# A small convolution on TensorE: two streams in four slots, or in three with half-height tiles

## The chip, the cores and the metric

The kernel runs on one core of a Trainium2 chip. The metric is the time of one execution on the device in microseconds (us), as the median over runs. TensorE multiplies matrices, VectorE (DVE), ScalarE (ACT) and GpSimd (POOL) do the elementwise work, SyncE (SP) issues most transfers. All data is float32.

## The reference, cut to what matters

`x` is 4 images of 128 channels, 96 x 96. They are group-normalised, and each image is read as four sequences of L = 9216 positions: by columns (V) and by rows (H), each forwards and backwards. Each sequence goes through the same block:

```python
t = grouped1x1(x, in_proj_w, in_proj_b, 4);  u, gate = t[:, :256], t[:, 256:]
u = conv1d(silu(u), dw_w, K=5)                 # depthwise, per channel
s = ssm_in_w @ u                               # 32 rows
a = clip(DMIN + (DMAX - DMIN) * sigmoid(ssm_delta_w @ u + b), ...)
bb, cc = tanh(ssm_b_w @ u + b), tanh(ssm_c_w @ u + b)
h = linear recurrence  h[n] = a[n] * h[n-1] + bb[n] * s[n]
u = u + ssm_out_w @ (cc * h + d * s)
u = grouped1x1(u * sigmoid(gate), mix_w, mix_b, 4)
y = out_proj_w @ u + out_proj_b
```

The four results are put back in image order, fused by a 128 x 512 matrix, and added to `x`.

## The kernel before

**Cut into pieces.** For each image there are two phases, V and then H (8 phases in all), and in each the forward and the backward sequence run together: stream f is s = 0, stream r is s = 1. A phase has NS = 6 steps, and a step four pairs: positions are taken modulo R = 4, and pair p holds the N = 384 positions of a step with remainder p, for both streams. So there are 192 pairs, t = 0 to 191, with p = t % 4. After them six `last_pair` calls empty the pipeline. The order of work on TensorE, VectorE, ScalarE and GpSimd is the order in which the program writes it; each engine takes its own list in that order and waits where its operands are not there.

**One pair, before.** `pair(t)` works on three ages of data at once:

- `rows`, twice: the first product for a unit of the next step (into the banks FRONT) and the gate product for a unit six pairs old (GATE). Tiles of the array are 32x32, sixteen side by side (eight for each purpose). ScalarE then makes the gate's tanh (L354) and the silu (L365).
- `taps`: the 5-tap convolution for the second half of the channels (j = 1). Tap 0 is a scaled copy on ScalarE into PSUM (L424), taps 1 to 4 are on VectorE (L426), both streams in one instruction.
- `conv(i, s)`, once for each stream: the same convolution for the first half of the channels, j = 0. These are laid out with the four remainders across the partitions, 32 channels each, in four groups g. The product with a banded 128x32 matrix for each g does all taps: k = 0 takes the remainders of this block of four positions, k = 1 those of the next. ScalarE copies the result to `u` (L410).
- `recurrence`: in the pairs with p = 0 and 1 half a step's scan on VectorE (L477); in every pair GpSimd makes an older pair's `z = cc * h + d * s` (L483 to L485, a product, a sum, a copy to the other partitions).
- `ssm_out`, `add_u` (L393), `gating` (L398, once for each stream): 32x32 products into the four banks 0 to 3, then VectorE adds `u` and multiplies by the gate.
- `proj(i)`: sixteen 128x32 products for bb, cc, a and s into two banks, then ScalarE: tanh for bb and a (L452), tap 0 of the next pair (L424), tanh for cc (L456), a copy of s (L458), s times d (L459); then GpSimd: two steps for a (L462, L463), bb * s (L464).
- `accumulate`, twice: mixing, output and fusing matrix in one (`w_fin`) on a finished unit, and VectorE adds the result into the image sum `acc` (L504 in V; in H L509 for f, which adds the bias too, and L511 for r). In the usual case the first call of a pair handles f, the second r. At the end of an image the sum is written out (L516) and the next image loaded (L521).

On TensorE a pair's order is: `rows`, `accumulate`, `conv` f, `rows`, `conv` r, `ssm_out`, `proj`, `accumulate`. All products are recorded under one line, L126 of the helper `mm`; they are told apart by their operands. A product in float32 is two instructions (two passes). PSUM has eight banks; which call uses which is fixed by the constants below. `conv` f and the second bank of `proj` share bank 5.

```python
SSM, TAPS, GATE, FRONT = 0, 0, (2, 3), (6, 7)
Y_1, CONV_F, CONV_R, PROJ, Y_2, SMALL = 4, 5, 4, (6, 5), 4, 7
```

At the start GpSimd builds the band matrices (32 products, L281). In the first six pairs no unit is old enough for the gate, `ssm_out` and `accumulate`.

Of the kernel before, what the change touches and what calls it, by code (L numbers as in the profile page):

```python
# [53 lines left out]
def conv_preact_kernel(  # L56
# [100 lines left out]
    NSC = L // SC  # L157
    stats = {}

    def stats_of(b):  # L160
# [4 lines left out]
    def stats_finish(b, newton):  # L165

        mv = sp.tile([P, 2], F32, tag="mv", name=f"mv_{b}")
        nc.vector.bn_aggr(mv, stats[b].rearrange("p c s -> p (c s)"))
        yield
        pm = bank(SMALL)  # L170
# [10 lines left out]
        pv = bank(SMALL)  # L181
# [20 lines left out]
        pb = bank(SMALL)  # L202
# [62 lines left out]

    band = wp.tile([P, R, 2, 4, 32], F32, name="band")
    w_fin = wp.tile([P, 4, 2, P], F32, name="w_fin")
    b_fin = wp.tile([P, 1], F32, name="b_fin")
    with tc.tile_pool(name="prep", bufs=1) as pp:
        w_dw = load(dw_v, [P, 4, 8], "w_dw", pp)  # L270
# [6 lines left out]
        for p in range(R):  # L277
            for k in range(2):
                for g in range(4):
                    m = R * k - p + R - 1  # L280
                    nc.gpsimd.tensor_scalar_mul(  # L281
                        band[:, p, k, g, :], id32, w_dw[:, g, m : m + 1]
                    )

# [40 lines left out]

    def rows(i, bi, banks=(FRONT, GATE)):

# [12 lines left out]
        for c in range(4):  # L340
            for j in range(2):
                if i is not None:
                    r = slice(32 * j, 32 * j + 32)
                    m, q = (c, g) if j else (g, c)
                    mm(bank(banks[0][j]), c, wn[r, 32 * m : 32 * m + 32], x_in[s][r, q, :],
# [17 lines left out]
        if i is not None:  # L363
# [7 lines left out]
            if g == 3:  # L371
                for j in range(2):
                    if un["st"] == 0:
                        r, q = (slice(0, P), slice(0, 2)) if j else (slice(0, 64), slice(0, 4))
                        nc.gpsimd.memset(sil[r, j, q, 0:1], 0.0)
                    if un["st"] == NS - 1:
                        r, q = (slice(0, P), slice(2, 4)) if j else (slice(64, P), slice(0, 4))
                        nc.gpsimd.memset(sil[r, j, q, N : N + 1], 0.0)
# [22 lines left out]

    def conv(i, s):

        un = units[i]
        sil = sils[un["step"]][:, s]
        pc = bank(CONV_R if s else CONV_F)
        for k in range(2):
            for g in range(4):
                mm(pc, g, band[:, un["p"], k, g, :], sil[:, 0, g, k : k + N], k == 0, k == 1)
        nc.scalar.copy(us[i][:, s, 0, :], pc[:, :N])  # L410

# [25 lines left out]

    def proj(i):

# [7 lines left out]
        for j in (1, 0):  # L447
            for bk, cols in zip(PROJ, ((qb, qb, qa, qa), (qc, qc, qs, qs))):
                for c in range(4):
                    mm(bank(bk), c, w_proj[:, j, cols[c]], us[i][:, c % 2, j, :], j == 1, j == 0)  # L450
        pa, pb = (bank(bk)[:, :N] for bk in PROJ)
        nc.scalar.activation(ta[:, p, :], pa, AF.Tanh, bias=b_proj[:, 0:1])  # L452
        if i + 2 < NU:
            new_u(i + 2)
            taps(i + 2, range(1))
        nc.scalar.activation(tb[0:64, p, :], pb[0:64, :], AF.Tanh, bias=b_proj[0:64, 1:2])  # L456
        st = wk.tile([P, N], F32, tag="s", name=f"s_{i}")
        nc.scalar.copy(st[0:64, :], pb[64:P, :])  # L458
        nc.scalar.activation(tb[64:P, p, :], pb[64:P, :], AF.Copy, scale=d_sb[64:P, :])  # L459
        a = ta[64:P, p, :]  # L460
        half = (DMAX - DMIN) / 2
        nc.gpsimd.tensor_scalar(a, a, half, DMIN + half, ALU.mult, ALU.add)  # L462
        nc.gpsimd.tensor_scalar(a, a, 0.9999, 0.0001, ALU.min, ALU.max)  # L463
        nc.gpsimd.tensor_mul(ta[0:64, p, :], st[0:64, :], ta[0:64, p, :])  # L464

    def scan(step, part):
# [4 lines left out]
        if part:  # L471
            init = ta[0:64, R - 1, N // 2 - 1 : N // 2]
        elif units[step * UB]["st"] == 0:
            init = 0.0
        else:
            init = scans[step - 1][0][0:64, R - 1, N - 1 : N]
        nc.vector.tensor_tensor_scan(  # L477
            seq[0:64, r], seq[64:P, r], seq[0:64, r], init, ALU.mult, ALU.add
        )

    def outputs(step, p):
        ta, tb = scans[step]
        nc.gpsimd.tensor_mul(ta[64:P, p, :], tb[0:64, p, :], ta[0:64, p, :])  # L483
        nc.gpsimd.tensor_add(tb[64:P, p, :], ta[64:P, p, :], tb[64:P, p, :])  # L484
        nc.gpsimd.tensor_copy(tb[0:64, p, :], tb[64:P, p, :])  # L485

    reload = []

    def accumulate(bu, bk):
        b, s, p, st = bu["b"], bu["s"], bu["p"], bu["st"]  # L490
        py = bank(bk)
        for j in range(2):
            for c in range(4):
                mm(py, c, w_fin[:, bu["dir"], j, 32 * c : 32 * c + 32], bu["v"][:, j, :],
                   j == 0, j == 1)
        y = py[:, :N]
        if s:
            y, p, st = y[:, ::-1], R - 1 - p, NS - 1 - st
        if bu["order"] == "V":
# [3 lines left out]
            y = y.rearrange("p (c r m) -> p m r c", r=R, m=M)  # L503
            nc.vector.tensor_add(part, y, part)  # L504
            return
        part = acc[:, bass.ts(st, LN), p, :]
        y = y.rearrange("p (h m) -> p h m", m=M)
        if s == 0:
            nc.vector.scalar_tensor_tensor(part, y, b_fin, part, ALU.add, ALU.add)  # L509
        else:  # L510
            nc.vector.tensor_add(part, y, part)  # L511
        if bu["st"] >= NS // 2 and bu["p"] == R - 1:
# [23 lines left out]
    def pair(t):  # L536
        i, k, bi = 2 * t, t % R, 2 * (t - LAG)
        front = i + UB if i + UB < NU else None
        back = bi if bi >= 0 else None
        rows(front, back)  # L540
        taps(i, range(1, 3))

        if waiting and (bi == 2 or (bi - 2) % (NU // B)):
            accumulate(waiting.pop(0), Y_1)
            if len(waiting) > 1 and units[bi]["st"] == 1:
                accumulate(waiting.pop(0), CONV_F)
# [12 lines left out]
        if back is not None:  # L559
            ssm_out(bi)  # L560
            add_u(bi)
            gating(bi, 0)
            if later:
                next(later[0], None)
            gating(bi, 1)
        proj(i)
        if waiting:
            accumulate(waiting.pop(0), Y_2)
        if back is not None:
# [108 lines left out]
```

## Time and profile before

| | |
|---|---|
| median of 3 runs | 2188.05 us (2185.58 to 2188.55) |
| the profiled execution | 2188.14 us, its span 2186.4 us |
| granted TensorE clock | 0.99 |
| instructions | 83167 |
| transfers | 133.84 MB, mean 61 GB/s |

The span runs from the first to the last instruction that the profiler recorded; the execution's own time is a little longer. Where the profile gives rows of the timeline, the first number is the start in us from the span's start, the second the duration in us; then engine, line, operation, what is written <- what is read, the tile's shape on the array (for products), operand shapes, and how many instructions were merged into the row. `[0.96 <-ACT ...]` is idle time of that engine ahead of the row, and what ended it. In rows of groups the figures are count, busy us in total, mean ns of one, and idle time ahead. "us" without a unit in the text below is microseconds.

### The profile page before, as it was taken

What the parts mean: (1) busy time and instruction counts of PE and PEld (TensorE: products, weight loads), DVE (VectorE), ACT (ScalarE), POOL (GpSimd) and SP (SyncE); (2) the same over time, 40 slices, a digit from 0 to 9 for tenths busy, and PEclk for the clock granted to TensorE, in tenths of its full rate; (3) what the DMA queues carried; (4) which work ended last, traced back from release to release, by engine and by line L of the source; (5) the groups of instructions that cost most, each with busy time, mean ns of one, the idle gap of its engine ahead of it and who ended that gap; (6) DMA issues with size and microseconds to landing.
All of it is one profiled execution on the core that took longest, in us unless ns stands there. A gap on an engine that the chain in (4) does not pass through costs nothing.

```text
span 2186.4 us, 83167 instructions
## 1 busy us (share of the span) xinstructions
PE 2136.5 (98%) x37072; PEld 724.7 (33%) x37072; DVE 1871.7 (86%) x1978; ACT 1576.3 (72%) x2899; POOL 1267.8 (58%) x1301
## 2 busy tenths in 40 slices
PE   5899999999999999999999999999999999999998
PEld 3233333333333333333333333333333333333333
DVE  3589998888888988888899899888888888888886
ACT  3677777777777777777777777777777777777762
POOL 2355656566655665666656565656566566655653
PEclk7899999999999999999999999999999999999999
DMA  5122121111441221111333221111134211111111
GB/s 154 39 57 64 49 57 35 42 35 45 141 134 50 56 57 48 36 42 35 100 107 114 57 64 42 41 36 42 35 100 135 55 36 43 35 42 35 35 49 68
DMA packets 83398, 133.84 MB, mean 61 GB/s; under 512 B 11616, under 2 KB 70624, under 8 KB 83040
## 3 DMA queue, kind: packets, MB, share of 16 engines
q1 hardware_dynamic: 81024, 127.64, 21.6%
q8 instruction: 291, 4.77, 0.9%
q10 hardware_dynamic: 2016, 0.88, 0.2%
q14 instruction: 67, 0.55, 0.1%
HBM read 109.60 MB, written 18.87 MB: 59 GB/s over the span
## 4 chain that ended last, share of the span: by engine, by line
PE 95%; DVE 2%; ACT 1%; DMA 1%; issue 1%; POOL 0%; ACTq 0%; SPq 0%; DVEq 0%
PE psum L126 95%; DVE psum L393 0%; DMA acc<-in_xr 0%; DVE gv L398 0%; DMA b_mix<-in_mix_b 0%; ACT psum L424 0%; ACT t L459 0%; DVE t L477 0%; ACT sil L365 0%; ACT gv L354 0%; DMA w_in<-in_in_wT 0%; DVE acc L511 0%; ACT t L452 0%; DVE psum L426 0%; ACT s L458 0%
## 5 line engine op out<-in xcount | busy, mean ns | idle before, releaser
L426 DVE SCALAR_TENSOR_TENSOR psum<-sil,w_tap,psum 128x768 f32<-128x768 f32 x576 | 585.7, 1017 | 49.6 <-ACT psum L424 42.2
L126 PE MATMUL psum<-sil,band 128*32 128x384 f32 x6144 | 576.7, 492 | 12.7 <-ACT t L459 10.4
L126 PE MATMUL psum<-gv,w_fin 128*32 128x384 f32 x6144 | 569.8, 490 | 0.5 <-DVE gv L398 0.5
L126 PE MATMUL psum<-u,w_proj 128*32 128x384 f32 x6144 | 536.0, 489 | 0.0
L462 POOL TENSOR_SCALAR t<-t 64x384 f32<-64x384 f32 x192 | 190.5, 992 | 568.7 <-ACT t L452 564.8
L354 ACT ACTIVATE gv<-psum,bnorm 128x384 f32<-128x384 f32 x768 | 403.1, 577 | 134.6 <-PE psum L126 129.9
L393 DVE TENSOR_TENSOR psum<-psum,u 128x1536 f32<-128x1536 f32 x192 | 339.2, 1767 | 170.4 <-PE psum L126 122.1
L452 ACT ACTIVATE t<-psum,b_proj 128x384 f32<-128x384 f32 x192 | 194.4, 1013 | 373.2 <-PE psum L126 373.2
L365 ACT ACTIVATE sil<-psum,bnorm 128x385 f32<-128x385 f32 x768 | 404.7, 586 | 18.0 <-PE psum L126 17.8
L126 PE MATMUL psum<-x_in,wn 32*32 32x384 f32 (+1 forms) x12288 | 405.8, 499 | 8.5 <-ACT t L452 3.0
L483 POOL TENSOR_TENSOR t<-t,t 64x384 f32<-64x384 f32 x192 | 235.6, 1227 | 220.0 <-DVE t L477 205.8
L398 DVE SCALAR_TENSOR_TENSOR gv<-gv,psum 128x768 f32<-128x768 f32 x384 | 350.8, 950 | 6.3
L126 PEld LDWEIGHTS psum<-sil,band 128*32 128x32 f32 x6144 | 181.0, 109 | 361.0 <-issue 218.8
L126 PEld LDWEIGHTS psum<-gv,w_fin 128*32 128x32 f32 x6144 | 181.7, 110 | 342.1 <-issue 222.7
L126 PEld LDWEIGHTS psum<-u,w_proj 128*32 128x32 f32 x6144 | 181.8, 110 | 335.1 <-issue 225.9
L464 POOL TENSOR_TENSOR t<-s,t 64x384 f32<-64x384 f32 x192 | 238.2, 1240 | 15.0 <-ACT s L458 0.7
L484 POOL TENSOR_TENSOR t<-t,t 64x384 f32<-64x384 f32 x192 | 235.3, 1226 | 15.1
L410 ACT COPY u<-psum 128x384 f32<-128x384 f32 x384 | 186.8, 487 | 44.9 <-PE psum L126 28.2
L126 PEld LDWEIGHTS psum<-x_in,wn 32*32 32x32 f32 x12288 | 115.5, 103 | 271.0 <-ACT sil L365 118.1
L426 DVE SCALAR_TENSOR_TENSOR u<-sil,w_tap,psum 128x768 f32<-128x768 f32 x192 | 194.9, 1015 | 6.8
L463 POOL TENSOR_SCALAR t<-t 64x384 f32<-64x384 f32 x192 | 191.4, 997 | 15.9
L126 PE MATMUL psum<-t,w_so 32*32 32x384 f32 x6144 | 188.9, 494 | 0.0
(70 smaller groups left out, 1204.5 us busy)
## 6 DMA issues: line engine op xcount, KB each, us to landing
x_in<-in_xs SPq DMA_DIRECT2D x96, 385.0 KB, 4.4
x_in<-in_xs SPq DMA_DIRECT2D x384, 96.2 KB, 2.4
acc<-in_xr SPq DMA_DIRECT2D x48, 384.0 KB, 4.3
out<-acc SPq DMA_DIRECT2D x48, 384.0 KB, 2.9
xs<-in_xr SPq DMA_DIRECT2D x72, 192.0 KB, 2.7
w_fuse<-in_fuse_wT ACTq DMA_DIRECT2D x1, 256.0 KB, 6.8
w_proj<-in_proj_wT ACTq DMA_DIRECT2D x1, 128.0 KB, 4.9
w_so<-in_ssm_out_wT ACTq DMA_DIRECT2D x1, 128.0 KB, 2.6
```

Source lines behind the costliest of these rows:

```text
L126: nc.tensor.matmul(o[r, : rhs.shape[-1]], lhsT, rhs, start=start, stop=stop, skip_group_check=True)
L354: nc.scalar.activation(gv[:, j, :], bank(banks[1][j])[:, :N], AF.Tanh, bias=gbn[:, 2 + j : 3 + j], scale=0.5,)
L365: nc.scalar.activation(sil[:, j, g, :], bank(banks[0][j])[:, : N + 1], AF.Silu, bias=bn[:, 1:2] if j else bn[:, 4 + g : 5 + g],)
L393: nc.vector.tensor_add(pz, pz, us[bi].rearrange("p s j n -> p (s j) n"))
L398: nc.vector.scalar_tensor_tensor(v, v, 1.0, pz, ALU.add, ALU.mult)
L426: nc.vector.scalar_tensor_tensor(us[i][:, :, 1, :] if k == K - 1 else part, src, w_tap[:, k : k + 1], part, ALU.mult, ALU.add,)
L452: nc.scalar.activation(ta[:, p, :], pa, AF.Tanh, bias=b_proj[:, 0:1])
L462: nc.gpsimd.tensor_scalar(a, a, half, DMIN + half, ALU.mult, ALU.add)
L463: nc.gpsimd.tensor_scalar(a, a, 0.9999, 0.0001, ALU.min, ALU.max)
L464: nc.gpsimd.tensor_mul(ta[0:64, p, :], st[0:64, :], ta[0:64, p, :])
L483: nc.gpsimd.tensor_mul(ta[64:P, p, :], tb[0:64, p, :], ta[0:64, p, :])
L484: nc.gpsimd.tensor_add(tb[64:P, p, :], ta[64:P, p, :], tb[64:P, p, :])
```

## The change

The two `conv` calls of a pair become one. Of the two band products of a stream (k = 0 and 1), one has zeros in at least half of its rows: for p = 0 and 1 only remainders 0 and 1 of the next block are reached (k = 1), for p = 2 and 3 only remainders 2 and 3 of this block (k = 0). That product ("small") is made on 64 rows. The remainders of stream r are laid out turned by two, so that its 64 rows are the other half, and the small products of f and r for the same g stand next to each other in the program, on different rows of the array and in different banks. The full products of both streams come first. The band matrices are now held for each stream, 64 products at the start.

The banks of PSUM alternate from pair to pair (`REST`). The order on TensorE becomes: `rows`, the new `conv`, `rows`, `accumulate`, `ssm_out`, `proj`, `accumulate`. Tap 0 of the next pair is issued after all of `proj`. In `proj`, cc and s change places: s is copied to `tb`'s lower half, and its product with d is made on GpSimd. The scan's and outputs' partitions are swapped accordingly. In `accumulate`, f's result is copied from PSUM by ScalarE (in H with the bias) to a new tile `ys` and added to `acc` by GpSimd; r's is added by VectorE as before.

```diff
-    SSM, TAPS, GATE, FRONT = 0, 0, (2, 3), (6, 7)
-    Y_1, CONV_F, CONV_R, PROJ, Y_2, SMALL = 4, 5, 4, (6, 5), 4, 7
+    SSM, TAPS, GATE = 0, 0, (2, 3)
+    REST = ((4, 5), (6, 7))
...
-    def conv(i, s):
+    def conv(i, banks):
         un = units[i]
-        sil = sils[un["step"]][:, s]
-        pc = bank(CONV_R if s else CONV_F)
-        for k in range(2):
+        sil, p = sils[un["step"]], un["p"]
+        small = 1 if p < 2 else 0
+
+        def part(s, k, g, r, start):
+            mm(bank(banks[s]), g, band[r, s, p, k, g, :], sil[r, s, 0, g, k : k + N],
+               start, not start)
+
+        for s in range(2):
             for g in range(4):
-                mm(pc, g, band[:, un["p"], k, g, :], sil[:, 0, g, k : k + N], k == 0, k == 1)
-        nc.scalar.copy(us[i][:, s, 0, :], pc[:, :N])
+                part(s, 1 - small, g, slice(0, P), True)
+        for g in range(4):
+            for s in range(2):
+                low = 64 * ((small + s + 1) % 2)
+                part(s, small, g, slice(low, low + 64), False)
+        for s in range(2):
+            nc.scalar.copy(us[i][:, s, 0, :], bank(banks[s])[:, :N])
...
     def proj(i, banks):
...
         nc.scalar.activation(ta[:, p, :], pa, AF.Tanh, bias=b_proj[:, 0:1])
-        if i + 2 < NU:
-            new_u(i + 2)
-            taps(i + 2, range(1))
-        nc.scalar.activation(tb[0:64, p, :], pb[0:64, :], AF.Tanh, bias=b_proj[0:64, 1:2])
-        st = wk.tile([P, N], F32, tag="s", name=f"s_{i}")
-        nc.scalar.copy(st[0:64, :], pb[64:P, :])
-        nc.scalar.activation(tb[64:P, p, :], pb[64:P, :], AF.Copy, scale=d_sb[64:P, :])
+        nc.scalar.copy(tb[0:64, p, :], pb[0:64, :])
+        nc.scalar.activation(tb[64:P, p, :], pb[64:P, :], AF.Tanh, bias=b_proj[64:P, 1:2])
...
-        nc.gpsimd.tensor_mul(ta[0:64, p, :], st[0:64, :], ta[0:64, p, :])
+        nc.gpsimd.tensor_mul(ta[0:64, p, :], tb[0:64, p, :], ta[0:64, p, :])
+        nc.gpsimd.tensor_scalar_mul(tb[0:64, p, :], tb[0:64, p, :], d_sb[0:64, :])
...
     def accumulate(bu, bk):
...
-        y = py[:, :N]
-        if s:
+        y, add = py[:, :N], nc.vector.tensor_add
+        if s == 0:
+            ys = wk.tile([P, N], F32, tag="ys", name=f"ys_{bu['id']}")
+            if bu["order"] == "V":
+                nc.scalar.copy(ys, y)
+            else:
+                nc.scalar.activation(ys, y, AF.Identity, bias=b_fin)
+            y, add = ys, nc.gpsimd.tensor_add
+        else:
             y, p, st = y[:, ::-1], R - 1 - p, NS - 1 - st
...
     def pair(t):
...
-        rows(front, back)
-        taps(i, range(1, 3))
-        if waiting and (bi == 2 or (bi - 2) % (NU // B)):
-            accumulate(waiting.pop(0), Y_1)
...
-        taps(i, range(3, K))
-        conv(i, 0)
+        front_banks, conv_banks = REST[t % 2], REST[1 - t % 2]
+        rows(front, back, (front_banks, GATE))
+        taps(i, range(1, K))
+        conv(i, conv_banks)
         recurrence(t)
...
+        if back is None:
+            first_tap(i + 2)
         if front is not None or back is not None:
-            rows(None if front is None else front + 1, None if back is None else bi + 1)
-        conv(i, 1)
+            rows(None if front is None else front + 1, None if back is None else bi + 1,
+                 (front_banks, GATE))
+        if waiting and (bi == 2 or (bi - 2) % (NU // B)):
+            accumulate(waiting.pop(0), conv_banks[0])
...
         if back is not None:
             ssm_out(bi)
             add_u(bi)
...
-        proj(i)
+        proj(i, (conv_banks[1], front_banks[0]))
+        if back is not None:
+            first_tap(i + 2)
         if waiting:
-            accumulate(waiting.pop(0), Y_2)
+            accumulate(waiting.pop(0), front_banks[1])
```

More of the change, by code (lines that the diff above doesn't have):

```diff
@@ L264, in conv_preact_kernel @@
     )
-    band = wp.tile([P, R, 2, 4, 32], F32, name="band")
+    band = wp.tile([P, 2, R, 2, 4, 32], F32, name="band")
     w_fin = wp.tile([P, 4, 2, P], F32, name="w_fin")
@@ L269, in conv_preact_kernel @@
     with tc.tile_pool(name="prep", bufs=1) as pp:
-        w_dw = load(dw_v, [P, 4, 8], "w_dw", pp)
+        w_dw = load(dw_v, [P, 2, 4, 8], "w_dw", pp)
         id32 = pp.tile([P, 32], F32, name="id32")
@@ L276, in conv_preact_kernel @@
             nc.gpsimd.tensor_copy(id32[r, :], ident[r, r])
-        for p in range(R):
-            for k in range(2):
[L279 to L283, printed above, removed]
+        for s in range(2):
+            for p in range(R):
+                for k in range(2):
+                    for g in range(4):
+                        m = R * k - p + R - 1
+                        nc.gpsimd.tensor_scalar_mul(
+                            band[:, s, p, k, g, :], id32, w_dw[:, s, g, m : m + 1]
+                        )
         w_out = load(out_w, [P, HID], "w_out", pp)
@@ L324, in conv_preact_kernel, with rows @@
     sils = {}
-    def rows(i, bi, banks=(FRONT, GATE)):
+    def rows(i, bi, banks):
         if i is not None:
@@ L436, in conv_preact_kernel, with proj @@
     qb, qc, qa, qs = (slice(MH * i, MH * (i + 1)) for i in range(4))
-    def proj(i):
+    def proj(i, banks):
         step, p = units[i]["step"], units[i]["p"]
@@ L475, in scan @@
         else:
-            init = scans[step - 1][0][0:64, R - 1, N - 1 : N]
+            init = scans[step - 1][0][64:P, R - 1, N - 1 : N]
         nc.vector.tensor_tensor_scan(
-            seq[0:64, r], seq[64:P, r], seq[0:64, r], init, ALU.mult, ALU.add
+            seq[64:P, r], seq[64:P, r], seq[0:64, r], init, ALU.mult, ALU.add
         )
@@ L503, in accumulate @@
             y = y.rearrange("p (c r m) -> p m r c", r=R, m=M)
-            nc.vector.tensor_add(part, y, part)
+            add(part, y, part)
             return
@@ L507, in accumulate @@
         y = y.rearrange("p (h m) -> p h m", m=M)
[L508 to L511, printed above, removed]
+        add(part, y, part)
         if bu["st"] >= NS // 2 and bu["p"] == R - 1:
@@ L561, in pair @@
             add_u(bi)
-            gating(bi, 0)
             if later:
+                small[0] = front_banks[1]
                 next(later[0], None)
-            gating(bi, 1)
-        proj(i)
+            for s in range(2):
+                gating(bi, s)
+        proj(i, (conv_banks[1], front_banks[0]))
+        if back is not None:
+            first_tap(i + 2)
         if waiting:
-            accumulate(waiting.pop(0), Y_2)
+            accumulate(waiting.pop(0), front_banks[1])
         if back is not None:
```

42 lines of the change are left out of this document (25 added, 17 removed).

## The prediction

> **What bounds the kernel now.** I read the busy shares and the chain of the page first, then one steady pair in the timeline, then the groups, then start and end. The page:
>
> ```profile
> PE 2136.5 (98%) x37072; PEld 724.7 (33%) x37072; DVE 1871.7 (86%) x1978; ACT 1576.3 (72%) x2899; POOL 1267.8 (58%) x1301
> ...
> PE 95%; DVE 2%; ACT 1%; DMA 1%; issue 1%; POOL 0%; ACTq 0%; SPq 0%; DVEq 0%
> ```
>
> TensorE ends the time over 95% of the span. A busy share doesn't say what a slot costs, so here is TensorE through one pair (timeline; start, duration, engine, line, operands, count), from one first call of `rows` to the next:
>
> ```profile
> 1110.40 0.94 PE L126 MATMUL psum<-x_in,wn 32*32 32x385 f32 x32
> 1111.28 1.50 PE L126 MATMUL psum<-gv,w_fin 128*32 128x384 f32 x16
> 1112.59 1.47 PE L126 MATMUL psum<-sil,band 128*32 128x384 f32 x16
> 1113.99 1.02 PE L126 MATMUL psum<-x_in,wn 32*32 32x385 f32 x32
> 1114.94 1.50 PE L126 MATMUL psum<-sil,band 128*32 128x384 f32 x16
> 1116.37 0.94 PE L126 MATMUL psum<-t,w_so 32*32 32x384 f32 x32
> 1117.24 2.79 PE L126 MATMUL psum<-u,w_proj 128*32 128x384 f32 x32
> 1119.85 1.47 PE L126 MATMUL psum<-gv,w_fin 128*32 128x384 f32 x16
> 1121.25 0.94 PE L126 MATMUL psum<-x_in,wn 32*32 32x385 f32 x32
> ```
>
> The pair takes 10.85. No row has an idle time behind it. Starts are what counts, since ends are modelled. `proj` runs 2.61 from start to start for four slots (a slot: eight instructions that fill the array, two passes over four column strips), so a slot is 0.65. `rows` and `ssm_out` (32x32 tiles, sixteen side by side) are one slot each, `accumulate` and each `conv` two: 3 + 4 + 4 + 4 = 15 slots, 9.79. The other 1.06 lies at the six changes of tile shape: before a narrower tile 0.10 to 0.13 (conv to `rows`: 1112.59 + 1.30 to 1113.99), before a wider one 0.22 to 0.30 (`rows` to conv: 1113.99 + 0.65 to 1114.94). First and last steady pair, by `ssm_out`:
>
> ```profile
> 112.09 0.94 PE L126 MATMUL psum<-t,w_so 32*32 32x384 f32 x32
> ...
> 2132.38 0.94 PE L126 MATMUL psum<-t,w_so 32*32 32x384 f32 x32
> ```
>
> That is 185 intervals (pairs 6 to 191) of 10.92 in the mean: 10.85 for an ordinary one, and some long ones at the phase borders that I leave as they are.
>
> **TensorE, part by part.** Removed: two band calls of two slots each. Added: two full slots (both streams) and one slot in which two 64x32 halves run side by side. So 14 slots, 9.13. Five of the six old changes of shape stay in kind (`rows` to conv 0.25, `rows` to `accumulate` 0.23, `accumulate` to `ssm_out` 0.13, `ssm_out` to `proj` 0.22, `accumulate` to `rows` 0.10). Two are new: 128x32 to 64x32 and 64x32 to 32x32. No row has a 64-row tile; both go to a narrower tile, so I take 0.12 each, and keep 0.10 to 0.30 each as bounds. Sum 9.13 + 0.93 + 0.24 = 10.30, bounds 10.26 to 10.66.
>
> The Trainium skill speaks against the extra shape: TensorEngine Tiling (Array Packing), Key Properties, says that changing the tiling mode drains the array, and TensorE: Matmul & The Clock Gate, Single matmul latency, puts a drain at roughly 175 ns. By that estimate the new pair of changes costs 0.35 and the sum below would be 20 us higher; the trace agrees that a change costs, at 0.10 to 0.30 with the narrowing ones at the low end.
>
> **Does another engine let TensorE run at 10.30?** The same pair elsewhere:
>
> ```profile
> 1117.54 1.77 DVE L393 TENSOR_TENSOR psum<-psum,u 128x1536 f32<-128x1536 f32 x1 [0.96 <-ACT sil L365]
> 1119.34 1.82 DVE L398 SCALAR_TENSOR_TENSOR gv<-gv,psum 128x768 f32<-128x768 f32 x2
> 1119.45 1.02 ACT L452 ACTIVATE t<-psum,b_proj 128x384 f32<-128x384 f32 x1 [1.90 <-PE psum L126]
> 1120.33 0.91 ACT L424 ACTIVATE psum<-sil,w_tap 128x768 f32<-128x768 f32 x1
> 1121.18 0.56 ACT L456 ACTIVATE t<-psum,b_proj 64x384 f32<-64x384 f32 x1
> 1121.46 0.56 DVE L511 TENSOR_TENSOR acc<-psum,acc 128x384 f32<-128x384 f32 x1 [0.29 <-PE psum L126]
> 1121.76 0.47 ACT L458 COPY s<-psum 64x384 f32<-64x384 f32 x1
> 1121.93 2.07 DVE L426 SCALAR_TENSOR_TENSOR psum<-sil,w_tap,psum 128x768 f32<-128x768 f32 x2
> 1122.26 0.57 ACT L459 ACTIVATE t<-psum,d_sb 64x384 f32<-64x384 f32 x1
> 1122.86 1.06 ACT L354 ACTIVATE gv<-psum,bnorm 128x384 f32<-128x384 f32 x2
> 1123.80 1.06 ACT L365 ACTIVATE sil<-psum,bnorm 128x385 f32<-128x385 f32 x2
> 1124.98 0.48 ACT L410 COPY u<-psum 128x384 f32<-128x384 f32 x1
> ```
>
> ScalarE. Removed: the scaled copy L459, 0.57. Added: the copy of f's result, 0.48 as L410 (with the bias about 0.56). Its load doesn't change; its order does: the first tap L424 moves behind the copy and the tanh of `proj`, and both conv copies now stand ahead of the second gate tanh. Counted from the start of `rows` (0): L452 starts at -1.80 (1119.45 against 1121.25; `proj` and the second `accumulate` still lie between). The next three follow at the old distances 0.88, 0.50, 0.58, and the tap takes 0.91: done at 1.07 (before: 1120.33 + 0.91, thus -0.01). Gate tanh 0.94 and silu 1.06 end at 3.07; the second `rows` wants its banks at 0.65 + 0.25 + 1.30 + 0.12 + 0.65 + 0.12 = 3.09. Two copies to 4.1, gate tanh 1.06 to 5.2; `ssm_out` wants those banks at 3.09 + 0.65 + 0.23 + 1.30 + 0.13 = 5.40. So ScalarE just fits, with 0.2 to spare; I cost it at nothing. Without that cover each tenth is a tenth a pair, 18 us.
>
> VectorE. Removed: the add of f (0.61 with bias). But all four taps now wait for the later tap 0: from 1.07, twice 2.07 to 5.25 with the hand-over. In the two pairs of four that hold a scan it comes next, then `add_u` and `gating`, whose banks the next `rows` writes. The scan and what GpSimd does to it, in the timeline and, last, in the answers by line (shortest, median, longest in ns):
>
> ```profile
> 1092.87 1.23 POOL L484 TENSOR_TENSOR t<-t,t 64x384 f32<-64x384 f32 x1
> 1093.98 1.81 DVE L477 TENSOR_TENSOR_SCAN t<-t,t 64x768 f32<-64x768 f32 x1
> 1094.16 1.93 POOL L485 COPY t<-t 64x384 f32<-64x384 f32 x1
> ...
> 2139.77 2.84 DVE L477 TENSOR_TENSOR_SCAN t<-t,t 64x768 f32<-64x768 f32 x1 [1.74 <-POOL t L464]
> 2139.81 1.19 POOL L483 TENSOR_TENSOR t<-t,t 64x384 f32<-64x384 f32 x1
> ...
> L477 DVE TENSOR_TENSOR_SCAN t<-t,t x40: 1808/1809/2841, 133.0 to 2139.8; 64x768 f32<-64x768 f32 x40
> L485 POOL COPY t<-t x192: 499/500/2052, 102.5 to 2161.0; 64x384 f32<-64x384 f32 x192
> ```
>
> Scan 1.81 to 7.06, `add_u` 1.77 and `gating` 1.82 with two hand-overs to 10.71: the next `rows` can write at 10.75, not at 10.30. The first scan pair of a step (p = 0) waits 0.45. The second doesn't: its tap 0 hangs on `proj`, which was not delayed, so its chain starts 0.45 earlier and ends at 10.30. Pairs p = 2, 3 have no scan (10.71 - 1.81 = 8.9). Further, scan and GpSimd shut each other out: the copy beside a scan took 1.93 instead of its median 0.50, and a scan that started with a GpSimd multiply took 2.84 instead of 1.81. GpSimd's three output steps reach p = 0's scan later than now, as a fourth step of `proj` stands ahead: L484 at about 4.5 to 5.7, across the scan's 5.25. I take 0.35 for it; bounds 0 and a whole multiply, 1.24. So p = 0 loses 0.8, the mean pair 0.20: 10.50.
>
> GpSimd. Prices, from the groups (count, busy us, mean ns) and, for the start, from the timeline:
>
> ```profile
> L462 POOL TENSOR_SCALAR t<-t 64x384 f32<-64x384 f32 x192 | 190.5, 992 | 568.7 <-ACT t L452 564.8
> L464 POOL TENSOR_TENSOR t<-s,t 64x384 f32<-64x384 f32 x192 | 238.2, 1240 | 15.0 <-ACT s L458 0.7
> 9.39 10.67 POOL L281 TENSOR_SCALAR band<-id,w_dw 128x32 f32<-128x32 f32 x32 [5.67 <-DMA w_dw<-in_dw_v]
> 46.23 2.57 PE L126 MATMUL psum<-sil,band 128*32 128x384 f32 x16
> ```
>
> Added per pair: a scale of 64x384, 0.99, and f's add over 128x384. No row has 128 partitions; nearest is L464, 1.24, and twice that, 2.48, is the upper end. Today's work is 1267.8 / 192 = 6.6, so 8.8, at most 10.1: under 10.50, though little at the top. Behind the scan of p = 1 the add comes late (outputs to about 10.3, add to 11.5) and the next `proj` steps queue behind it; nothing needs those before the next step's scan. SP issues the same transfers in the same order; the output DMA waits for both adds, off the path. The 32 more band products cost GpSimd 10.7 at the start; it is hidden, as the present ones end at 20.06 and the first conv starts at 46.23; without that cover, 10.7.
>
> Start and end, in the timeline:
>
> ```profile
> 44.30 2.00 PE L126 MATMUL psum<-x_in,wn 32*32 32x385 f32 x16 [1.20 <-ACT sil L365]
> 65.32 2.65 PE L126 MATMUL psum<-sil,band 128*32 128x384 f32 x16 [1.39 <-ACT t L459]
> 105.50 0.94 PE L126 MATMUL psum<-x_in,wn 32*32 32x385 f32 x32 [0.43 <-ACT t L452]
> 2144.31 0.61 DVE L509 SCALAR_TENSOR_TENSOR acc<-psum,b_fin,acc 128x384 f32<-128x384 f32 x1
> ```
>
> The first six pairs take 61.2 because conv waits until ScalarE has emptied bank 5 that `proj` filled (L452 to the end of L459: 0.88 + 0.85 + 0.58 + 0.50 + 0.57 = 3.38). With alternating banks conv needs two readers less (0.88 + 0.50 + 0.56 = 1.94), and the band work is 0.65 shorter: 2.0 a pair, 12 us (bounds 6 and 17). In the last six pairs f's add, 0.61, leaves VectorE's chain while its new path runs beside: 2 us.
>
> **Sum.** 185 x (10.85 - 10.50) = 65; 65 + 12 + 2 = 79. The profiled execution took 2188.14 (span 2186.4), the median of the three runs is 2188.05; 2188.1 - 79 = 2109, told as 2110.
>
> **Rivals.**
> A. VectorE's wait is hidden (tap 0 earlier than reckoned, no collision): 10.30, 185 x 0.55 + 14 = 116, 2072. For it: ScalarE sits idle 1.90 before L452 now. Against: the 1.07 is a plain sum of rows.
> B. The lock decides: p = 0's scan loses a whole multiply, 0.45 + 1.24 = 1.69, 0.42 a pair, 10.72: 2188 - 24 - 14 = 2150. For it the 2.84 row; against, such scans have a median of 1.81. SBUF — State Buffer, Who interferes with whom, of the Trainium skill, states that a VectorE instruction with two SBUF inputs and a GpSimd one that reads SBUF exclude each other for a whole instruction; the trace agrees, with 1.93 against 0.50. A slower GpSimd add (2.48) or 0.25 more on ScalarE ends near here too.
> C. The other side: the halves don't overlap, so the change doesn't do what it says. Conv then takes four slots with one shape more: 10.95 (VectorE's 10.75 hidden), 185 x 0.10 - 14 = +5, 2193; with both new changes at 0.30, 11.31, 2260; I take 2205. It decides once about 0.6 of the 0.65 is lost. Against: sixteen 32x32 tiles on four row groups fit in one slot, 1116.37 to 1117.24, two row groups in one column strip included. For: no 64-row tile has run here.
>
> **Chances and range.** Forecast 0.45 (2090 to 2135), A 0.25, B 0.19, C 0.11. About 0.2% (4.4 us) is what a measurement here can tell from no change. C at its low end is within it: same 0.03, slower 0.08; the other three are faster: 0.89. Leaving C out and A's and B's far ends in: 2060 to 2160.
>
> **What would show it.** TensorE: 14 slots, the 64x32 group 0.65 long and its two changes near 0.12; ordinary pairs 10.30, each p = 0 pair about 11.1 with `rows` waiting for VectorE's L398 line. Tap 0 ending 1.07 after `rows` starts. Scans longer than 1.81 in p = 0 only. First six pairs near 49. It is wrong if the 64x32 group takes 1.3, if GpSimd's add passes 2 us, or if `ssm_out` or the second `rows` waits for ScalarE.

## The result, and the profile after

The changed kernel takes 2120.02 us in the median (2118.82 to 2122.77), the one before 2188.30 beside it: ratio 0.969, 95% interval 0.9673 to 0.9707. The profiled execution took 2122.77 (span 2121.0). The saving is 68 in the medians and 65.4 between the two profiled executions (after the change, the profiled one is the slowest of its four); 79 was forecast.

The page after, busy shares and the chain:

```profile
PE 2074.4 (98%) x37072; PEld 666.1 (31%) x37072; DVE 1814.4 (86%) x1786; ACT 1557.4 (73%) x2899; POOL 1732.4 (82%) x1717
PE 92%; DVE 3%; ACT 2%; POOL 1%; DMA 1%; issue 0%; ACTq 0%; SPq 0%; POOLq 0%; DVEq 0%
```

TensorE still ends the time; GpSimd went from 58% to 82% without becoming the bound. TensorE through an ordinary pair after, in the timeline, from one first call of `rows` to the next:

```profile
1083.59 0.95 PE L129 MATMUL psum<-x_in,wn 32*32 32x385 f32 x32
1084.46 2.31 PE L129 MATMUL psum<-sil,band 128*32 128x384 f32 x32
1086.70 1.01 PE L129 MATMUL psum<-x_in,wn 32*32 32x385 f32 x32
1087.64 1.50 PE L129 MATMUL psum<-gv,w_fin 128*32 128x384 f32 x16
1089.07 0.94 PE L129 MATMUL psum<-t,w_so 32*32 32x384 f32 x32
1089.94 2.79 PE L129 MATMUL psum<-u,w_proj 128*32 128x384 f32 x32
1092.55 1.47 PE L129 MATMUL psum<-gv,w_fin 128*32 128x384 f32 x16
1093.95 0.94 PE L129 MATMUL psum<-x_in,wn 32*32 32x385 f32 x32
```

The pair takes 10.36, against 10.85. The row named 128*32 at 1084.46 holds all 32 band instructions, the 64-row ones too (the timeline merges neighbours). It runs 2.24 to the next `rows`: three slots are 1.96 (a slot is 2.61 / 4 = 0.65 by `proj`, 1089.94 to 1092.55), and 0.28 goes to the two new changes of shape. By the whole pair it is 0.30: 10.36 less 14 slots (9.13) and the five old changes (0.93).

Which pairs are longer is read from the starts of `ssm_out`, here from five neighbours, with those of the first and the last steady pair around them:

```profile
98.72 2.44 PE L129 MATMUL psum<-t,w_so 32*32 32x384 f32 x32
...
878.98 0.94 PE L129 MATMUL psum<-t,w_so 32*32 32x384 f32 x32
889.34 0.94 PE L129 MATMUL psum<-t,w_so 32*32 32x384 f32 x32
900.16 0.95 PE L129 MATMUL psum<-t,w_so 32*32 32x384 f32 x32
910.56 0.94 PE L129 MATMUL psum<-t,w_so 32*32 32x384 f32 x32
920.92 0.94 PE L129 MATMUL psum<-t,w_so 32*32 32x384 f32 x32
...
2068.97 0.94 PE L129 MATMUL psum<-t,w_so 32*32 32x384 f32 x32
```

The intervals are 10.36, 10.82, 10.40 and 10.36. The long one is the pair with p = 0; over the step the mean is 10.49. Across all 185 intervals the mean is (2068.97 - 98.72) / 185 = 10.65, so longer ones stand elsewhere. Inside the pair with p = 0, on the other engines:

```profile
883.86 0.94 PE L129 MATMUL psum<-x_in,wn 32*32 32x385 f32 x32
884.01 0.91 ACT L440 ACTIVATE psum<-sil,w_tap 128x768 f32<-128x768 f32 x1
888.01 1.24 POOL L500 TENSOR_TENSOR t<-t,t 64x384 f32<-64x384 f32 x1
889.18 1.81 DVE L494 TENSOR_TENSOR_SCAN t<-t,t 64x768 f32<-64x768 f32 x1
889.33 2.67 POOL L501 TENSOR_TENSOR t<-t,t 64x384 f32<-64x384 f32 x1
891.02 1.77 DVE L399 TENSOR_TENSOR psum<-psum,u 128x1536 f32<-128x1536 f32 x1
892.82 1.82 DVE L404 SCALAR_TENSOR_TENSOR gv<-gv,psum 128x768 f32<-128x768 f32 x2
894.22 1.41 PE L129 MATMUL psum<-x_in,wn 32*32 32x385 f32 x32
894.69 0.24 PEld L129 LDWEIGHTS psum<-x_in,wn 32*32 32x32 f32 x30 [0.34 <-DVE gv L404]
```

The next `rows` begins at 894.22 and stops: its loads sit idle until VectorE's `gating` (L404 here) has let go of the banks at 894.64, and the row takes 1.41 instead of 0.94. The scan itself took 1.81, though GpSimd's multiply (L500) still had 0.07 to run when it began. GpSimd's add (L501), which came 0.15 later, stood instead: it took 2.67, where the same add takes 1.22 beside other work.

In the profile before, GpSimd's second output step (L484, at 1092.87 in the rows of the prediction) comes 4.18 after the first `rows` of its pair, also one with p = 0; after the change that step (L501) comes 5.47 after `rows` (889.33 against 883.86). The `rows` of the pair before the change:

```profile
1088.69 0.94 PE L126 MATMUL psum<-x_in,wn 32*32 32x385 f32 x32
```

The new operations, from the groups (count, busy us, mean ns, idle time ahead):

```profile
L129 PE MATMUL psum<-sil,band 64*32 64x384 f32 x3072 | 168.9, 497 | 0.0
L476 POOL TENSOR_SCALAR t<-t,d_sb 64x384 f32<-64x384 f32 x192 | 240.5, 1253 | 19.8
L528 POOL TENSOR_TENSOR acc<-ys,acc 128x384 f32<-128x384 f32 x96 | 117.5, 1224 | 6.8 <-DVE psum L442 0.6 <-DMA x_in<-in_xs 0.2 <-DMA xs<-in_xr 0.2
L532 POOL TENSOR_TENSOR acc<-ys,acc 128x384 f32<-128x384 f32 x96 | 97.6, 1017 | 17.1 <-ACT ys L519 10.9
```

Where the 65.4 came from:

| | before | after | saved | forecast |
|---|---|---|---|---|
| to the first `ssm_out` | 112.09 | 98.72 | 13.4 | 12 |
| 185 intervals, ordinary part | 10.835 each | 10.4925 each | 63.4 | 65 |
| 185 intervals, what the long ones add | 15.8 | 29.1 | -13.3 | 0 |
| last `ssm_out` to the end of the span | 54.0 | 52.0 | 2.0 | 2 |

The "ordinary part" is the mean of the step's repeating four intervals; the third row is the sum of all intervals less 185 times that mean. The first interval counts among the long ones: after the change it is 11.78, as the first `ssm_out` comes early and takes 2.44. Below, the excess of an interval is what it takes beyond the median of its own p; summed over all intervals it is 15.1 before and 29.5 after.

### The profile page after: what moved, and what is told of

It is laid out like the page before. It is cut to its first block, busy times and chain, and to the rows that moved or that the text cites. A ratio compares the mean times of both kernels' runs of the same rounds, so it can differ in the third digit from the quotient of the medians.

```text
span 2121.0 us, 83902 instructions
## 1 busy us (share of the span) xinstructions
PE 2074.4 (98%) x37072; PEld 666.1 (31%) x37072; DVE 1814.4 (86%) x1786; ACT 1557.4 (73%) x2899; POOL 1732.4 (82%) x1717
## 4 chain that ended last, share of the span: by engine, by line
PE 92%; DVE 3%; ACT 2%; POOL 1%; DMA 1%; issue 0%; ACTq 0%; SPq 0%; POOLq 0%; DVEq 0%
PE psum L129 91%; DVE t L494 1%; DVE psum L399 1%; DVE gv L404 1%; ACT t L468 0%; ACT sil L370 0%; DMA acc<-in_xr 0%; POOL t L475 0%; DMA b_mix<-in_mix_b 0%; ACT psum L440 0%; DVE psum L442 0%; POOL t L476 0%; POOL t L500 0%; POOL t L473 0%; POOL t L474 0%
## 5 line engine op out<-in xcount | busy, mean ns | idle before, releaser
L359 ACT ACTIVATE gv<-psum,bnorm 128x384 f32<-128x384 f32 x768 | 403.2, 577 | 91.8 <-PE psum L129 79.3
L468 ACT ACTIVATE t<-psum,b_proj 128x384 f32<-128x384 f32 x192 | 193.9, 1010 | 369.6 <-PE psum L129 356.6
L129 PE MATMUL psum<-sil,band 128*32 128x384 f32 (+1 forms) x6144 | 445.4, 495 | 0.2
L399 DVE TENSOR_TENSOR psum<-psum,u 128x1536 f32<-128x1536 f32 x192 | 339.2, 1767 | 122.3 <-PE psum L129 62.8
L129 PE MATMUL psum<-x_in,wn 32*32 32x384 f32 (+1 forms) x12288 | 432.0, 498 | 7.2 <-DVE gv L404 4.2
L500 POOL TENSOR_TENSOR t<-t,t 64x384 f32<-64x384 f32 x192 | 242.6, 1264 | 155.6 <-DVE t L494 146.3
L404 DVE SCALAR_TENSOR_TENSOR gv<-gv,psum 128x768 f32<-128x768 f32 x384 | 349.4, 950 | 6.4
L501 POOL TENSOR_TENSOR t<-t,t 64x384 f32<-64x384 f32 x192 | 290.6, 1514 | 15.0
L473 POOL TENSOR_SCALAR t<-t 64x384 f32<-64x384 f32 x192 | 187.1, 975 | 100.2 <-ACT t L468 88.6
L476 POOL TENSOR_SCALAR t<-t,d_sb 64x384 f32<-64x384 f32 x192 | 240.5, 1253 | 19.8
L475 POOL TENSOR_TENSOR t<-t,t 64x384 f32<-64x384 f32 x192 | 237.0, 1234 | 15.4
L129 PEld LDWEIGHTS psum<-sil,band 128*32 128x32 f32 (+1 forms) x6144 | 114.5, 107 | 318.1 <-issue 276.3
L129 PEld LDWEIGHTS psum<-x_in,wn 32*32 32x32 f32 x12288 | 124.5, 103 | 286.0 <-ACT sil L370 117.6
L129 PE MATMUL psum<-t,w_so 32*32 32x384 f32 x6144 | 198.0, 493 | 4.2 <-POOL t L500 3.9
L474 POOL TENSOR_SCALAR t<-t 64x384 f32<-64x384 f32 x192 | 184.2, 960 | 15.9
```

Source lines behind the costliest of these rows:

```text
L129: nc.tensor.matmul(o[r, : rhs.shape[-1]], lhsT, rhs, start=start, stop=stop, skip_group_check=True)
L359: nc.scalar.activation(gv[:, j, :], bank(banks[1][j])[:, :N], AF.Tanh, bias=gbn[:, 2 + j : 3 + j], scale=0.5,)
L399: nc.vector.tensor_add(pz, pz, us[bi].rearrange("p s j n -> p (s j) n"))
L404: nc.vector.scalar_tensor_tensor(v, v, 1.0, pz, ALU.add, ALU.mult)
L475: nc.gpsimd.tensor_mul(ta[0:64, p, :], tb[0:64, p, :], ta[0:64, p, :])
L476: nc.gpsimd.tensor_scalar_mul(tb[0:64, p, :], tb[0:64, p, :], d_sb[0:64, :])
```

## The experiments

Ratios are to the kernel before.

**Full-height small products.** The new order and banks stay, the small products get all 128 rows again:

```diff
-                low = 64 * ((small + s + 1) % 2)
-                part(s, small, g, slice(low, low + 64), False)
+                part(s, small, g, slice(0, P), False)
```

> The small band products run on all 128 rows (the rows added hold zeros in the band), so the conv takes four slots and the array keeps one shape there; everything else as after the change. Theory T (the gain of an ordinary pair is the saved slot less the extra change of shape): conv to second rows call 2.24 becomes 2.58 + 0.11, the ordinary pair 10.36 becomes 10.81, VectorE's wait of p = 0 is hidden, 185 x (10.81 - 10.49) = +59 on 2120: 2180. Rival N (the gain comes from the new order, the banks and VectorE's relief, not from the half-height tiles): 2120 to 2130.

2186.6, 0.9998 (0.9988 to 1.0007). In its timeline the band work runs 2.76 to the next `rows`, four slots (2.61) and a change:

```profile
900.91 2.82 PE L129 MATMUL psum<-sil,band 128*32 128x384 f32 x32
903.67 0.98 PE L129 MATMUL psum<-x_in,wn 32*32 32x385 f32 x32
```

The pair is back at 10.85. The first `ssm_out` comes at 102.27, 9.8 sooner than before. The long intervals lose 7 of that again (an excess of 22.2 against 15.1), and the ordinary ones, 10.86 in the mean against 10.84, most of the rest. The net gain belongs to the half-height tiles; order, banks and the moved adds bring nothing on their own.

**Both halves on the same rows.** Still eight 64-row products, but r's uses the rows that f's uses. There r's band is zero, so r's share of the small product is left out:

```diff
-                low = 64 * ((small + s + 1) % 2)
+                low = 64 * ((small + 1) % 2)
```

> The changed kernel, with f's and r's small products on the same 64 rows, so r's is made from the wrong half of its remainders. Theory T (the slot is saved because the two halves lie on different rows): the 64x32 group takes 1.3, the pair 11.0, VectorE's wait is hidden, 185 x 0.51 = 94 more than 2120, with the first six pairs 2218. Rival Q (a product of half height is simply quicker, whatever its rows): 2120.

2212.88, 1.0108 (1.0091 to 1.0125).

```profile
891.41 2.94 PE L129 MATMUL psum<-sil,band 128*32 128x384 f32 x32
894.29 1.00 PE L129 MATMUL psum<-x_in,wn 32*32 32x385 f32 x32
```

2.88 from start to start instead of 2.24: one slot more, with the same instructions and tile shapes. The slot is saved because the two halves stand on different rows of the array; in both kernels they go to different banks, and one bank for both was not tried. This is what the forecast's third rival would have looked like; it was priced at 2193 to 2260.

**Order of the halves.** All four of f, then all four of r:

```diff
-        for g in range(4):
-            for s in range(2):
+        for s in range(2):
+            for g in range(4):
```

> The eight half-height products in the order f, f, f, f, r, r, r, r instead of f, r alternating. Theory A (TensorE starts products in program order and looks only a few ahead, so that f's two passes fill one half of the rows for two passes before r's begin): conv takes 0.65 more, the pair 11.0, 2120 + 185 x 0.5 = 2213. Theory B (it pairs whatever finds its rows free): 64x32 group 0.65 as now, 2120.

2120.18, 0.9698 (0.9677 to 0.9719), no change. Instructions for the two row halves need not alternate: four for one half followed by four for the other overlap as well.

**Tap 0 sooner.** Is the 0.46 of p = 0 the chain from tap 0? Tap 0 moves ahead of the last tanh of `proj`:

```diff
         nc.scalar.copy(tb[0:64, p, :], pb[0:64, :])
+        if i >= 2 * LAG:
+            first_tap(i + 2)
         nc.scalar.activation(tb[64:P, p, :], pb[64:P, :], AF.Tanh, bias=b_proj[64:P, 1:2])
...
-        if back is not None:
-            first_tap(i + 2)
```

> Tap 0 of the next pair is issued between proj's copy of s and its tanh for cc, 0.58 sooner. Theory T (p = 0 waits 0.46 because VectorE's chain hangs on tap 0): the wait goes, all pairs 10.36, 185 x 0.13 = 24 less, 2096. Rival B (the tanh that moves back empties the bank that f's full band product of the next pair fills; it ends at about 1.05 after rows starts, the product wants the bank at 0.87): every pair waits about 0.2, 10.55, 2131.

2119.47, 0.969 (0.9676 to 0.9705), no change in the time, but not for want of effect: the p = 0 interval fell from 10.82 to 10.62 in the median, and the pairs with p = 2 and 3 rose from 10.36 to 10.46. The loads of the band products wait for the bank that the delayed tanh (L472) empties, and begin 0.95 after `rows` instead of 0.87:

```profile
881.64 0.94 PE L129 MATMUL psum<-x_in,wn 32*32 32x385 f32 x32
...
881.97 0.57 ACT L472 ACTIVATE t<-psum,b_proj 64x384 f32<-64x384 f32 x1
...
882.59 0.16 PEld L129 LDWEIGHTS psum<-sil,band 128*32 128x32 f32 x8 [0.71 <-ACT t L472]
882.60 2.30 PE L129 MATMUL psum<-sil,band 128*32 128x384 f32 x32
```

With p = 1 (10.43 to 10.47) the four pairs of a step are 0.05 longer together, 2 us over the kernel; the excess of the long ones is 5 us smaller in the profile (24.2 against 29.5). So the ordinary pairs cancel, as the next run confirms.

**The same, with r's full products first** (that bank then is wanted later):

```diff
-        for s in range(2):
+        for s in (1, 0):
             for g in range(4):
                 part(s, 1 - small, g, slice(0, P), True)
```

> Tap 0 sooner as in x3, and r's full band products ahead of f's, so that the product that wants proj's second bank comes 0.65 later. Theory T (x3 stood still because two things cancelled: the scan pair's wait shrank to about 0.2, and every pair got 0.10 from the bank that the late tanh empties): the 0.10 goes, pairs of 10.36 and one of about 10.55 in four, mean 10.41, 185 x 0.08 = 15 less than 2120: 2105. Rival C (ScalarE's whole chain is the limit at 10.46): 2119.

2111.97, 0.9652 (0.9639 to 0.9665). Ordinary pairs are at 10.36 again, p = 0 at 10.72 in the median: the gain is real but smaller than the 2105 hoped for. The scan now meets GpSimd, whose multiply (L502) has 0.46 left when it begins. Its timeline, and then the scans by line (shortest, median, longest in ns):

```profile
882.30 1.23 POOL L502 TENSOR_TENSOR t<-t,t 64x384 f32<-64x384 f32 x1
883.07 2.07 DVE L496 TENSOR_TENSOR_SCAN t<-t,t 64x768 f32<-64x768 f32 x1
...
L496 DVE TENSOR_TENSOR_SCAN t<-t,t x40: 1814/2114/2440, 118.4 to 2065.3; 64x768 f32<-64x768 f32 x40
```

The scans with p = 0 (but for each phase's first) take 2.11 in the median, where after the change they took 1.81:

```profile
L494 DVE TENSOR_TENSOR_SCAN t<-t,t x40: 1812/1814/2907, 120.7 to 2076.5; 64x768 f32<-64x768 f32 x40
```

So the collision that the forecast charged to p = 0 exists, but needs a scan that starts with more than 0.2 of a GpSimd instruction still to run; in the ordinary pair after the change 0.05 to 0.18 were left, and the scan lost nothing.

**f added by VectorE from PSUM**, as before the change, in both orders V and H (the cut shows H; in V the plain add on VectorE does it):

```diff
...
-        add(part, y, part)
+        if s:
+            add(part, y, part)
+        else:
+            nc.vector.scalar_tensor_tensor(part, y, b_fin, part, ALU.add, ALU.add)
```

> f's result is added by VectorE straight from PSUM, as before the change; ScalarE's copy and GpSimd's add are gone. Theory T (VectorE's chain tap 0, taps, scan, add_u, gating sets the wait of the scan pairs, and f's add, 0.56 to 0.61, now stands inside it ahead of add_u): p = 0 waits 1.0 instead of 0.46, p = 1 waits 0.45 instead of 0.07, mean pair 10.36 + 0.36 = 10.72, 185 x 0.23 = 43 more than 2120: 2163. Rival S (VectorE is busy 86% and has room; TensorE alone counts): 2120.

2151.81, 0.9833 (0.9819 to 0.9846), against 2163 expected. The p = 0 interval is 11.31 in the median; f's add stands in VectorE's chain, between scan and `add_u` (L399):

```profile
901.32 1.81 DVE L494 TENSOR_TENSOR_SCAN t<-t,t 64x768 f32<-64x768 f32 x1
...
903.16 0.62 DVE L528 SCALAR_TENSOR_TENSOR acc<-psum,b_fin,acc 128x384 f32<-128x384 f32 x1
903.70 1.75 DVE L399 TENSOR_TENSOR psum<-psum,u 128x1536 f32<-128x1536 f32 x1
```

Here the pairs with p = 0 and 1 pay (11.31 and 10.58), the others stay at 10.36; p = 1 lost 0.22 where 0.45 was expected. That VectorE's chain is the one that p = 0 waits for is shown from both sides: tap 0 sooner took 0.20 off, and `add_u` 0.54 later (2.38 after the scan's start instead of 1.84) costs 0.49. It also shows that the moved add is needed for the gain: without it 36 us are left.

**No GpSimd add of f at all** (its share of the output is left out, in both orders):

```diff
-        add(part, y, part)
+        if s:
+            add(part, y, part)
```

> GpSimd's add of f is left out (ScalarE's copy stays), so f's share is missing from the sum; 1.0 to 1.2 us less for GpSimd in each pair. Theory T (GpSimd's added work is hidden): 2120 within 4. Rival L (GpSimd at 82% makes others wait, through the scan's exclusion or a late output): 2105 or less. Rival M (with the add gone GpSimd's output steps come sooner and meet the scan of p = 0): 2125 to 2150.

2117.23, 0.9677 (0.9664 to 0.969): at most 3 us, within the intervals. In the profiled executions the difference of 2.6 lies behind the last `ssm_out` (49.3 to the end instead of 52.0). In the steady pairs the add is hidden, as forecast.

**A fifth buffer for the gate.**

```diff
-            gv = wk.tile([P, 2, N], F32, tag="gv", bufs=4, name=f"gv_{bu['id']}")
+            gv = wk.tile([P, 2, N], F32, tag="gv", bufs=5, name=f"gv_{bu['id']}")
```

> Five buffers for the gate tile gv instead of four. Theory G (in the pairs after an image's start the accumulate that frees a gate tile comes one call later on TensorE than the tanh that wants it, which makes intervals of 11.95 and 13.24): about 1.2 us less in each of two or three pairs of three images, 2120 - 9 = 2111. Rival O (these intervals come from the order of ScalarE's copy and the scan alone): 2120.

2115.41, 0.9671 (0.9656 to 0.9685): 4.6 faster, half of what was expected, with intervals that overlap; the traces tell more. It bears on the unforecast row of the table. After the change, at the start of the second image, in the timeline:

```profile
627.50 1.50 PE L129 MATMUL psum<-gv,w_fin 128*32 128x384 f32 x16
628.93 2.16 PE L129 MATMUL psum<-t,w_so 32*32 32x384 f32 x32
629.07 1.05 ACT L359 ACTIVATE gv<-psum,bnorm 128x384 f32<-128x384 f32 x2 [1.71 <-PE psum L129]
631.02 2.79 PE L129 MATMUL psum<-u,w_proj 128*32 128x384 f32 x32
```

At each image's start one `accumulate` is skipped, and finished units are worked off one call later. The gate's tanh (L359) has no free buffer until `accumulate` has read one; after the change that first `accumulate` stands behind the second `rows` on TensorE (before, ahead of it). ScalarE sits idle for 1.71, and half of `ssm_out` waits for the banks that the tanh is to read: `proj` starts 2.09 after `ssm_out` instead of 0.87. The two intervals there are 11.95 and 13.24 (before: 10.82 and 13.02); with a fifth buffer 11.29 and 12.25. Over the three image starts (six intervals each) the excess falls from 14.0 to 8.7.

**All of these together** (tap 0 sooner, r first, five buffers):

> x7 and five gate buffers together. If both act apart: 2105 less the 5 that x4 brought, 2100. If the gate buffers help only where tap 0 is late: 2105.

2104.06, 0.9617 (0.9604 to 0.963), 7.9 below the kernel with four buffers. The buffer brings more here than alone: the excess at the image starts falls from 16.8 to 8.7.

**p = 0's output steps later**, on top of that: GpSimd makes them behind f's add, to keep them off the scan.

```diff
-    def recurrence(t):
+    def recurrence(t, late=False):
         i, k = 2 * t, t % R
-        if k < 2 and 0 <= t // R - 1 < NU // UB:
+        if not late and k < 2 and 0 <= t // R - 1 < NU // UB:
             scan(t // R - 1, k)
-        if 0 <= i - 10 < NU:
+        if 0 <= i - 10 < NU and (late or k or i >= NU):
...
+        if k == 0:
+            recurrence(t, late=True)
```

> x6 with GpSimd's three output steps of p = 0 written behind f's add, so that GpSimd stands idle (it waits for ys) when the scan of p = 0 starts. Theory T (what is left of p = 0's wait, 0.35, is mostly the scan standing still for GpSimd's running multiply: 2.07 in place of 1.81): p = 0 falls from 10.71 to about 10.45, 185 / 4 x 0.26 = 12 less than 2104: 2092. Rival D (the later outputs push GpSimd's steps of proj onto p = 1's scan instead): 2104 or more.

2157, 0.9856 (0.984 to 0.9873), where 2092 was expected. The rival's "2104 or more" covers the number but not the mechanism, as the pairs with p = 1 stay at 10.36. The scan is back at 1.81, but ScalarE's first tanh of the next `proj` (L468) waits for GpSimd's output step (L503):

```profile
907.19 0.99 ACT L468 ACTIVATE t<-psum,b_proj 128x384 f32<-128x384 f32 x1 [3.72 <-POOL t L503]
```

Tile `ta` of a step has two buffers, and the new step takes the one that this output step is the last to read. The p = 0 interval became 11.9. A third buffer was not tried.

**The statistics step between the two gatings.** At the end of an image's V phase (the expectations call it the image's end) VectorE makes the next image's means (L177 to L183), now ahead of both `gating`s. After the change, in the timeline:

```profile
288.53 2.88 DVE L494 TENSOR_TENSOR_SCAN t<-t,t 64x768 f32<-64x768 f32 x1
288.56 1.24 POOL L501 TENSOR_TENSOR t<-t,t 64x384 f32<-64x384 f32 x1
...
293.25 0.16 DVE L177 COPY mean<-psum 128x1 f32<-128x1 f32 x1
...
293.77 0.92 DVE L183 TENSOR_SCALAR gm<-gmask,mean 128x4 f32<-128x4 f32 x1
294.58 1.81 DVE L404 SCALAR_TENSOR_TENSOR gv<-gv,psum 128x768 f32<-128x768 f32 x2
...
296.44 0.93 PE L129 MATMUL psum<-x_in,wn 32*32 32x384 f32 x30 [0.73 <-DVE gv L404]
```

The scan is lengthened by GpSimd, 1.33 pass from the first of the statistics to `gating`, and `rows` waits; the interval is 12.73. The edit was tried twice, on the kernel with the late outputs and on the one without:

```diff
+            gating(bi, 0)
             if later:
                 small[0] = front_banks[1]
                 next(later[0], None)
-            for s in range(2):
-                gating(bi, s)
+            gating(bi, 1)
```

> x9, and at an image's end the statistics step stands between the two gatings on VectorE, as before the change, not ahead of both. Theory S (the long intervals at an image's end come from the tap that waits for the first gating): 1 to 4 less than x9. Rival: the second gating still ends as late and the next rows wait for it: as x9.

2153.31, 0.984 (0.9826 to 0.9855), 4 under the one without; the intervals overlap.

> x6 with the statistics step of an image's end between the two gatings. Theory S (x10 lay 4 below x9 for this reason): 2104 - 4 = 2100. Rival: the 4 came from elsewhere or from scatter: 2104.

2100.75, 0.9608 (0.9595 to 0.9621), the fastest of all: 19 below the changed kernel and 86 below the one before. The times alone don't show that the last edit gains its 3, as its interval overlaps that of the kernel without it. The traces place it: between these two profiled executions the excess at the three V phase ends falls from 9.9 to 6.6, and all else changes by 0.2; on the kernel with the late outputs it falls from 9.3 to 6.9 there.

## Why the prediction was right, and where its steps were off

- **14 slots.** Right: the two halves share one slot (0.65), and taking the row split away costs just that slot.
- **The new changes of shape**, 0.12 each: they cost 0.28 to 0.30 together, about 0.15 each. Base 10.36 instead of 10.30, 185 x 0.06 = 11 us lost. It was within the bounds. The Trainium skill, TensorE: Matmul & The Clock Gate, Single matmul latency, has a drain at roughly 175 ns. As an estimate for the pair, 0.35, this lies about as far above what was measured as my 0.24 lies below.
- **p = 0 waits for VectorE's chain from tap 0**, 0.45: right in place and size. Tap 0 ended 1.05 after `rows` in an ordinary pair (1.07 forecast), and p = 0 loses 10.82 - 10.36 = 0.46. That the size is so close owes a little to luck: the end of VectorE's chain (`gating` off the banks 10.83 after `rows`, 10.75 forecast) and the base both moved up by 0.06 to 0.08. The pair with p = 1 loses 0.04 to 0.07, not nothing.
- **Collision with GpSimd**, 0.35: wrong in the ordinary step. GpSimd's second output step began 5.47 after `rows`, and I had 4.5. That was too early by the rows before: 4.18 and a scale of 0.99 make 5.17, still ahead of the scan at 5.25. The scale then took 1.25, with 0.06 to 0.10 for each hand-over in GpSimd's queue, and so the scan, at 5.32, came ahead of the step. SBUF — State Buffer, Who interferes with whom, of the Trainium skill, says that issue order decides which of the two stands. The trace agrees here, where the scan is recorded 0.15 ahead and the add stood (2.67). At 288.53 the scan is recorded only 0.03 ahead, and there it was the scan that stood (2.88, beside an add of 1.24); so close together the recorded starts don't tell the order. In sum this term and the one on shapes cancel, 10.4925 against 10.50, and that is luck.
- **GpSimd's prices.** The scale was too low (1.25 for 0.99). The add of f was 1.0 to 1.2, just below the 1.24 to 2.48: here 128 partitions cost no more than 64. Hidden, as the run without it shows.
- **Start and end.** 13.4 for 12 and 2.0 for 2. The start's first six pairs take 51.1 by `rows` (43.28 to 94.38) and save 10.1, not 12; they begin 1.0 sooner, and the first regular pair gives 2.3 up to its `ssm_out`, 1.4 of which its interval gives back. Not all of the 10.1 need be the banks: the granted clock in these pairs was 0.85 before and 0.94 after, and the two are not separated.
- **The failed step** is "some long ones at the phase borders that I leave as they are". They grew from 15.8 to 29.1, nearly all of the 13.6 missing between the profiled executions. By the excess in these two executions, the three image starts add 14.0 (before 6.6), the three ends of a V phase 12.6 (before 6.3), the first interval 1.4 (before nothing). Two mechanisms were seen. At image starts it is the wait for a gate buffer: a fifth takes the 14.0 to 8.7. At V phase ends it is VectorE's chain: with tap 0 sooner the scan there takes at most 1.91 instead of 2.9, and the 12.6 became 9.9; with the statistics back between the two gatings it became 6.6, about what it was before. The scan's part is the less certain one, as it hangs on a few hundredths: with the fifth buffer alone, two of the three scans escape, and the sum there is 11.2.

Of the rivals, "VectorE's wait is hidden" (2072) is refuted by the 0.46, "the lock decides" (2150) by scans of 1.81, and "the halves don't overlap" by the 2.24 from conv to `rows`, which becomes 2.88 on the same rows.

## What to carry to other kernels

Where a product has zeros in half of its rows, two such products on opposite row halves of the array run in the time of one (here into different banks); the price to set against it is a change of shape at each end, about 0.15 here. When an order is changed, walk through the irregular pairs (ends and starts of phases and images) by the same sum as the ordinary ones: a call that moves behind another shifts every buffer that it frees and every wait behind it, and here the irregular pairs took a sixth of the gain. A step moved earlier frees one wait and makes another: look which bank or buffer its new neighbour holds.

## What the runs showed of the hardware

- Eight 64x32 products on two row halves take one slot (0.65) whether their instructions alternate between the halves or not; on the same half they take two.
- A tensor-by-scalar on GpSimd with a scalar for each partition from memory (L476) takes 1.25 at 64x384, those with constants (L473, L474) 0.96 to 0.98. An add over 128x384 takes 1.02 to 1.22, no more than one over 64x384.
- A scan takes 1.81 alone (1.75 to 1.82). One that began with up to 0.2 of a GpSimd instruction left to run took no longer, in all 293 cases of the kept traces; with 0.46 left it took 2.07, with 0.82 left 2.42, the rest less 0.2.
- Where a GpSimd add or multiply began 0.051 to 0.16 after a scan by the recorded starts, it stood and took 2.6 to 2.8 instead of 1.2. Where it began 0.047 or less after the scan, the scan stood and took 2.82 to 2.95. No case in the 14 traces crosses this border.
